# Attention by halves beside networks by quarters, the third network in two lanes, the last beside the end of the delta rule

## The chip, the core and the metric

The kernel runs on one core of a Trainium2 chip, in float32 nearly throughout. The metric is the device time of one execution, in microseconds. The engines are PE (matrix products; PEld is its weight load), DVE (elementwise work and reductions), ACT (functions and copies), POOL (a second elementwise engine) and SP, whose queue issues every DMA of this kernel.

## The reference, cut to what matters

`x` is 1024 rows of 256. Six stages follow each other; each reads what the one before wrote.

```python
x = x + 0.5 * net0(layernorm(x))      # ternary weights 704 wide, with scales
x = x + attention(layernorm(x))       # 16 heads of 128, 4 key heads, window of 64, rotary,
                                      # relu(softmax1 - lam * softmax2), renormalized
x = x + 0.5 * net0(layernorm(x))      # the same weights again
x = x + 0.5 * net1(layernorm(x))      # weights looked up: lut[idx], 688 wide
x = x + delta_rule(x)                 # 16 heads, a recurrence over the rows
x = x + 0.5 * net1(layernorm(x))
# net(y) = (silu(y Wg * sg) * (y Wu * su)) Wd * sd
```

Layer norm and network treat every row by itself. The attention of a row reads keys of the row itself and of 63 rows before it. The delta rule goes through the rows in order, for each head.

## The kernel before, in words

The rows lie in SBUF as 8 tiles of 128 (`x`). `xnT` holds them normalized and transposed, with 64 columns of padding ahead. A half is four tiles, 512 columns of `xnT`.

**Networks.** `layernorm` (L100) takes a half: `bn_stats` and `bn_aggr` on DVE, a square root on ACT (L110), a reciprocal, the scaled tile `xn` (L116), two transposes on PE for each tile and one copy (L122). `ffn` (L124) takes a half through six chunks of 128 hidden units: PE makes `pg` and `pu` with 512 columns each (L135), ACT takes Silu (L140 with the scales, L152 without) and DVE multiplies (L143 or L153). Then for each tile PE makes `po` out of six products of 256 columns (L160), and DVE adds half of it to `x` (L167). `pg` and `pu` have two PSUM banks each.

**Table weights.** `lut_weights` (L169) is a generator. For each of 14 blocks of index (344 or 256 columns) it issues a load of `ix` and then 19 DVE steps: bit masks (L184, L189), selections among two table values (L195) and predicated copies (L208). `lut_steps` runs some steps of it after each chunk of the first network and after each tile of the attention.

**Attention.** All values come first (L237), with shifted copies of them by DMA (L245, L247). Then four groups of heads follow. For each, the keys and four queries are projected (L253) and rotated for both halves (`rope`: DVE L262, L263, L265, POOL L266). Then come eight tiles: PE adds the window mask and the scores in a PSUM tile of two banks (L291, L302), DVE takes the maxima (L313) and negates them (L314), ACT makes the exponentials (L319), DVE the differences (L336), ACT the relu (L339), POOL the renormalization (L346), PE the transposes (L349), the product with the values `pa` (L354) and the output `po` (L365), and DVE adds to `x` (L372). `pa` and `po` have a bank each.

**Delta rule.** `delta_rule` (L509) begins with narrow projections of all rows (L566, L578). Then it works through 16 pairs of tiles (four groups of heads, four pairs each) in rounds: `prepare` two pairs ahead (L641 are its projections), `triangle` one ahead, `solve`, `invert` and `values` for the pair itself, `advance` and `emit` for the pair behind; `emit` ends with a sum into `x` (L1104). `weave` gives each of these lanes a stretch of the round, and orders their steps by it. Small transfers to and from DRAM on SP's queue stand between `triangle`, `solve` and `invert`.

**What sets the order.** The program's text gives each engine a list, and a scheduler of the tile framework, which has a timeline of its own, reorders it before it is built. A tile in a pool has a number of buffers; an instruction that takes one again waits for the last reader. The stages of before follow each other in the text: both halves of the first network, the whole attention, both halves of the second and third networks, the delta rule, both halves of the last network. The table weights of the third network are written to DRAM (L457) and read again at the end (L473).

Of the kernel before, what the change touches and what calls it, by code (L numbers as in the profile page):

```python
# [59 lines left out]

@with_exitstack
def macaron_kernel(ctx, tc, out, a):
    nc = tc.nc
# [17 lines left out]
    nc.vector.memset(ones, 1.0)  # L81

# [3 lines left out]
    def stage_pools(stack):  # L86

        pool = lambda name, bufs, **kw: stack.enter_context(
            tc.tile_pool(name=name, bufs=bufs, reuse_waits="tile", **kw)
        )  # L90
        return dict(
            ln=pool("ln", 4),
            lnp=pool("lnp", 2, space=PSUM),
            ffh=pool("ffh", 2),
            ffs=pool("ffs", 3),
            ffp=pool("ffp", 2, space=PSUM),
            ffo=pool("ffo", 2, space=PSUM),
        )

    def layernorm(pools, hf):  # L100

        lp = pools["ln"]
        mv = lp.tile([P, 4, 2], F32, name="mv")
        for i in range(4):
            st = lp.tile([P, 6], F32, name="st")
            nc.vector.bn_stats(st, x[:, 4 * hf + i, :])
            nc.vector.bn_aggr(mv[:, i, :], st)
        sd = lp.tile([P, 4], F32, name="sd")
        nc.vector.tensor_scalar_add(sd, mv[:, :, 1], LN_EPS)
        nc.scalar.activation(sd, sd, AF.Sqrt)  # L110
        rs = lp.tile([P, 4], F32, name="rs")
        nc.vector.reciprocal(rs, sd)
        for i in range(4):
            n = 4 * hf + i
            xn = lp.tile([P, D], F32, name="xn")
            nc.vector.tensor_scalar(  # L116
                xn, x[:, n, :], mv[:, i, 0:1], rs[:, i : i + 1], ALU.subtract, ALU.mult
            )
            pt = pools["lnp"].tile([P, KC, P], F32, name="pt")
            for c in range(KC):  # L120
                nc.tensor.transpose(pt[:, c, :], xn[:, c * P : (c + 1) * P], ident)
            nc.scalar.copy(xnT[:, :, PAD + n * P : PAD + (n + 1) * P], pt)  # L122

    def ffn(pools, hf, wg, wu, wd, inter, scaled):  # L124

        cols = slice(PAD + hf * 512, PAD + (hf + 1) * 512)
        hT = pools["ffh"].tile([P, NI, 512], F32, name="hT")
        for ic in range(NI):
            n = min(P, inter - ic * P)
            cs = slice(ic * P, ic * P + n)  # L130
            pg = pools["ffp"].tile([P, 512], F32, name="pg")
            pu = pools["ffp"].tile([P, 512], F32, name="pu")
            for w, ps in ((wg, pg), (wu, pu)):
                for c in range(KC):
                    nc.tensor.matmul(  # L135
                        ps[:n], lhsT=w[:, c, cs], rhs=xnT[:, c, cols], start=(c == 0), stop=(c == KC - 1)
                    )
            sg = pools["ffs"].tile([P, 512], F32, name="sg")
            if scaled:
                nc.scalar.activation(  # L140
                    sg[:n], pg[:n], AF.Silu, scale=pp[:n, C_GS + ic : C_GS + ic + 1]
                )
                nc.vector.scalar_tensor_tensor(  # L143
                    hT[:n, ic, :],
                    pu[:n],
                    pp[:n, C_US + ic : C_US + ic + 1],
                    sg[:n],
                    ALU.mult,
                    ALU.mult,
                )  # L150
            else:
                nc.scalar.activation(sg[:n], pg[:n], AF.Silu)  # L152
                nc.vector.tensor_mul(hT[:n, ic, :], pu[:n], sg[:n])  # L153
            lut_steps(1024)
        for i in range(4):
            t = 4 * hf + i
            po = pools["ffo"].tile([P, D], F32, name="po")
            for ic in range(NI):
# [4 lines left out]
                    rhs=wd[:n, ic, :],  # L163
# [3 lines left out]
            nc.vector.scalar_tensor_tensor(x[:, t, :], po, 0.5, x[:, t, :], ALU.mult, ALU.add)  # L167

    def lut_weights(pool):  # L169
# [7 lines left out]
        for src, dst in (("gate_idx", w1g), ("up_idx", w1u), ("down_idx", w1d)):  # L177
            for c in range(dst.shape[1]):
                for c0 in range(0, dst.shape[2], I1 // 2):
                    n = min(I1 // 2, dst.shape[2] - c0)  # L180
                    ix = pool.tile([P, n], I32, name="ix", tag="ix", bufs=2)
                    nc.sync.dma_start(out=ix, in_=a[src][c * P : (c + 1) * P, c0 : c0 + n])
# [30 lines left out]
    lut = iter(())  # L213

    def lut_steps(columns):

        while columns > 0:
            got = next(lut, None)
            if got is None:
                return  # L220
            columns -= got

    def attention(wpool):
        win = wpool["win"]
        with tc.tile_pool(name="aqk", reuse_waits="tile", bufs=2) as qp, tc.tile_pool(name="av", reuse_waits="tile", bufs=1
        ) as vp, tc.tile_pool(name="as", reuse_waits="tile", bufs=2) as sp, tc.tile_pool(name="asm", reuse_waits="tile", bufs=4
        ) as small, tc.tile_pool(name="ap", reuse_waits="tile", bufs=2, space=PSUM
        ) as pj, tc.tile_pool(name="asc", reuse_waits="tile", bufs=2, space=PSUM) as psc, tc.tile_pool(name="aout", reuse_waits="tile", bufs=1, space=PSUM
        ) as pao:


            v = vp.tile([P, 2 * NT, NKV * HD], F32, name="v")
            nc.gpsimd.memset(v[0:64, 0, :], 0.0)
            for n in range(NT):
                pv = pj.tile([P, 512], F32, name="pv", tag="pj")
                for c in range(KC):
                    nc.tensor.matmul(  # L237
                        pv,
                        lhsT=xnT[:, c, PAD + n * P : PAD + (n + 1) * P],
                        rhs=wpool["wv"][:, c, :],  # L240
                        start=(c == 0),
                        stop=(c == KC - 1),
                    )
                nc.scalar.copy(v[:, 2 * n + 1, :], pv)
                nc.sync.dma_start(out=v[64:128, 2 * n, :], in_=v[0:64, 2 * n + 1, :])  # L245
                if n < NT - 1:
                    nc.sync.dma_start(out=v[0:64, 2 * n + 2, :], in_=v[64:128, 2 * n + 1, :])  # L247

            def rope(dst, w, hcol, hf):

                pr = pj.tile([P, 512], F32, name="pr", tag="pj")
                for c in range(KC):
                    nc.tensor.matmul(  # L253
                        pr,
                        lhsT=w[:, c, hcol : hcol + HD],
                        rhs=xnT[:, c, PAD + hf * 512 : PAD + (hf + 1) * 512],
                        start=(c == 0),
                        stop=(c == KC - 1),
                    )
                cs = slice(hf * 512, (hf + 1) * 512)  # L260
                rot = sp.tile([P, 512], F32, name="rot")
                nc.vector.tensor_mul(rot[0:64], pr[64:128], wpool["sin"][64:128, cs])  # L262
                nc.vector.tensor_mul(rot[64:128], pr[0:64], wpool["sin"][0:64, cs])  # L263
                runs = lambda ap: ap.rearrange("p (w t) -> p w t", t=64)
                nc.vector.tensor_mul(dst, runs(pr), runs(wpool["cos"][:, cs]))  # L265
                nc.gpsimd.tensor_add(dst, dst, runs(rot))  # L266

            for g in range(NKV):
                kT = qp.tile([P, PAD + T], F32, name="kT")
                nc.gpsimd.memset(kT[:, 0:PAD], 0.0)  # L270

                qTs = []
                for hf in range(2):
                    qT = qp.tile([P, 2, NT, 2, 64], F32, name="qT", bufs=3)
                    qTs.append(qT)
                    kh = kT[:, PAD + hf * 512 : PAD + (hf + 1) * 512]
                    rope(kh.rearrange("p (w t) -> p w t", t=64), wpool["wk"], g * HD, hf)
                    for h in range(HG):
                        rope(
                            qT[:, h // 2, :, h % 2, :],  # L280
                            wpool["wq"],
                            (g * HG + h) * HD,
                            hf,
                        )
                lam = wpool["lam"][:, 2 * g : 2 * g + 2].unsqueeze(2).to_broadcast([P, 2, 2])
                for n in range(NT):


                    ps = psc.tile([P, 2, 4, P], F32, name="ps")
                    for s in range(2):  # L290
                        nc.tensor.matmul(  # L291
                            ps[:, s].rearrange("p b k -> p (b k)"),
                            lhsT=wpool["idb"],
# [92 lines left out]
    with tc.tile_pool(name="w0", bufs=1, side="right") as w0p:  # L386
# [12 lines left out]
        with tc.tile_pool(name="wa", bufs=1) as wap, tc.tile_pool(  # L399
# [24 lines left out]
            with ExitStack() as st:  # L424
                pools = stage_pools(st)
                for hf in range(2):
                    layernorm(pools, hf)
# [833 lines left out]
```

## Time and profile before

| | us |
|---|---|
| median of 3 runs (1783.14 to 1787.38) | 1785.18 |
| the profiled execution | 1795.66 |
| its span, first to last instruction | 1793.8 |
| PE busy | 1532.6 |
| DVE busy | 1186.9 |
| ACT busy | 831.3 |
| POOL busy | 526.4 |

Mean granted clock of PE over the span: 0.897.

The span is cut by first and last instructions of some lines:

| | begins | ends |
|---|---|---|
| first network, with its loads and norms | 0 | 109.0 (first L262) |
| attention, first rope to last sum | 109.0 | 439.4 (last L372) |
| second and third networks, narrow projections | 439.4 | 599.6 (first L641) |
| delta rule, first projection to last sum | 599.6 | 1731.2 (last L1104) |
| rest of the last network | 1731.2 | 1793.8 |

To read a row of a stretch: its two ends, its length, then busy time and count of instructions for PE, PEld, DVE, ACT and POOL, the granted PE clock (1.00 is full), the share of the DMA engines and GB/s. To read a row of a group: line, engine, operation, names of output and inputs with shapes, count, then busy time and mean ns of one, then the engine's idle time ahead of them and what ended it. One float32 matmul shows as two records. Busy times of one engine overlap by a few per cent where rows are added.

### The profile page before, as it was taken

Reading aid. Unit: us, or ns where it says so; the run is one execution under the profiler, and the core shown is the slowest. Engines: PE = TensorE matmul, PEld = TensorE weight load, DVE = VectorE, ACT = ScalarE, POOL = GpSimd, SP = SyncE. Lnnn points to the kernel's source line nnn. Section 1 sums busy time; section 2 is a strip of 40 time slices with the busy share of each in tenths; the row PEclk is TensorE's granted clock in tenths of the full one; section 3 lists DMA queues with packets and bytes.
Section 4 is the critical chain, followed back from the end, with each engine's and each line's share of the span. In section 5 each row is a group of like instructions: output and inputs, shape, how many; then the busy total and the mean of one; then the engine's idle time right before and its main releaser. Section 6 shows DMA issues by size and latency. Waiting matters only on the chain.

```text
span 1793.8 us, 33380 instructions
## 1 busy us (share of the span) xinstructions
PE 1532.6 (85%) x13152; PEld 1107.1 (62%) x13152; DVE 1186.9 (66%) x2569; ACT 831.3 (46%) x1981; POOL 526.4 (29%) x470
## 2 busy tenths in 40 slices
PE   7886868777999766789989889898999898998879
PEld 3434445545555555667767677677778776776745
DVE  3999977584232357667678678876768877877221
ACT  2117273746122344536645645654665564563320
POOL 0022223231001034335434434433434442543100
PEclk9997989889999766789889989989889988989989
DMA  7020000002002001021111121102120120111100
GB/s 241 32 54 26 3 19 1 1 1 66 0 0 47 1 7 23 10 52 28 24 15 43 21 56 22 30 12 44 38 50 15 22 47 9 40 24 23 56 0 24
DMA packets 150348, 54.94 MB, mean 31 GB/s; under 512 B 116784, under 2 KB 142704, under 8 KB 149936
## 3 DMA queue, kind: packets, MB, share of 16 engines
q1 hardware_dynamic: 150192, 52.81, 12.8%
q8 instruction: 104, 1.70, 0.4%
q14 instruction: 52, 0.43, 0.1%
HBM read 39.11 MB, written 11.70 MB: 28 GB/s over the span
## 4 chain that ended last, share of the span: by engine, by line
PE 41%; DVE 26%; ACT 11%; DMA 9%; issue 6%; POOL 4%; SPq 3%; another core or an unknown queue 1%; DVEq 0%; POOLq 0%; ACTq 0%
PE ps L641 5%; DMA dm<-ml 4%; PE po L160 4%; PE pg L135 3%; PE pu L135 3%; DVE kq L813 3%; ACT e L319 3%; PE pm L791 2%; PE pr L253 2%; DVE k L655 2%; PE pg L700 2%; PE px L1101 2%; DVE other L195 2%; PE po L365 2%; DVE other L208 2%
## 5 line engine op out<-in xcount | busy, mean ns | idle before, releaser
L819 POOL TENSOR_TENSOR k<-k,d 128x512 f32<-128x512 f32 x96 | 149.7, 1559 | 312.2 <-PE pm L791 190.6
L791 PE MATMUL pm<-kq,k 128*64 128x64 f32 x3072 | 133.5, 235 | 29.9 <-POOL kq L742 11.5
L791 PEld LDWEIGHTS pm<-kq,k 128*64 128x64 f32 x3072 | 113.3, 146 | 62.0 <-issue 40.0
L813 DVE TENSOR_TENSOR kq<-kq,d 128x1024 f32<-128x1024 f32 x96 | 130.8, 1363 | 17.8 <-PE pm L791 6.7
L319 ACT ACTIVATE e<-ps,nm 128x128 f32<-128x128 f32 x256 | 91.5, 397 | 63.6 <-DVE nm L314 62.3
L655 DVE SCALAR_TENSOR_TENSOR k<-ps,pp,k 128x256 f32<-128x256 f32 x192 | 84.7, 473 | 27.0 <-ACT k L653 25.5
L655 DVE SCALAR_TENSOR_TENSOR q<-ps,pp,q 128x256 f32<-128x256 f32 x192 | 86.2, 478 | 22.7 <-ACT q L653 20.0
L655 DVE SCALAR_TENSOR_TENSOR v<-ps,pp,v 128x256 f32<-128x256 f32 x192 | 87.5, 474 | 19.8 <-ACT v L653 18.5
L253 PE MATMUL pr<-xnT,wq 128*128 128x512 f32 x128 | 64.7, 641 | 22.1 <-DVE nm L314 10.6
L641 PE MATMUL ps<-xnT,wv 128*128 128x259 f32 x256 | 79.5, 439 | 2.7 <-DVE v L655 1.5
L983 PE MATMUL dz<-mz,zt 64*64 64x32 f32 x768 | 74.9, 230 | 8.0 <-ACT mz L976 8.0
L991 PE MATMUL dz<-zt,mz 64*64 64x32 f32 x1024 | 81.4, 234 | 0.0
L641 PE MATMUL ps<-xnT,wq 128*128 128x259 f32 x256 | 78.6, 442 | 0.4 <-DVE ss L681 0.2
L365 PE MATMUL po<-wo,oT 128*128 128x256 f32 x256 | 64.1, 394 | 13.7 <-ACT oT L362 12.4
L991 PEld LDWEIGHTS dz<-zt,mz 64*64 64x64 f32 x1024 | 67.3, 147 | 12.4 <-issue 10.6
L1101 PE MATMUL px<-wdo,oT 128*128 128x256 f32 x256 | 70.4, 421 | 5.1 <-ACT oT L1097 5.1
L641 PE MATMUL ps<-xnT,wk 128*128 128x259 f32 x256 | 71.8, 418 | 1.0 <-ACT k L653 0.5
L742 POOL TENSOR_TENSOR kq<-q,ge 128x1024 f32<-128x1024 f32 x16 | 51.3, 3209 | 70.3 <-PE pso L1073 40.0
L653 ACT ACTIVATE q<-ps,pp 128x256 f32<-128x256 f32 x64 | 30.4, 474 | 89.1 <-PE ps L641 86.5
L968 PE MATMUL pmz<-z,mt 64*64 64x64 f32 x1024 | 56.1, 233 | 18.0 <-DMA z<-z 13.7
L968 PEld LDWEIGHTS pmz<-z,mt 64*64 64x64 f32 x1024 | 42.9, 140 | 44.4 <-issue 17.8
L708 ACT ACTIVATE gy<-pg,pp 128x256 f32<-128x256 f32 x64 | 29.4, 474 | 85.4 <-PE pg L700 67.5
(215 smaller groups left out, 3953.5 us busy)
## 6 DMA issues: line engine op xcount, KB each, us to landing
zt<-zt SPq DMA_DIRECT2D x32, 256.0 KB
dm<-ml SPq DMA_DIRECT2D x64, 64.0 KB
z<-z SPq DMA_DIRECT2D x64, 64.0 KB
wq<-in_aWq SPq DMA_DIRECT2D x1, 2048.0 KB
wo<-in_aWo SPq DMA_DIRECT2D x1, 2048.0 KB
wk<-in_dWk SPq DMA_DIRECT2D x4, 512.0 KB
wq<-in_dWq SPq DMA_DIRECT2D x4, 512.0 KB
wv<-in_dWv SPq DMA_DIRECT2D x4, 512.0 KB
```

The lines of the kernel that those rows point to most:

```text
L135: nc.tensor.matmul(ps[:n], lhsT=w[:, c, cs], rhs=xnT[:, c, cols], start=(c == 0), stop=(c == KC - 1))
L253: nc.tensor.matmul(pr, lhsT=w[:, c, hcol : hcol + HD], rhs=xnT[:, c, PAD + hf * 512 : PAD + (hf + 1) * 512], start=(c == 0), stop=(c == KC ...
L319: nc.scalar.activation(e[:, s, j, :], ps[:, s, j, :], AF.Exp, bias=nm[:, 4 * s + j : 4 * s + j + 1], scale=SUB**-0.5, accum_out=z[:, s, j ...
L365: nc.tensor.matmul(po, lhsT=oT[:, h, :], rhs=wpool["wo"][:, g * HG + h, :], start=(h == 0), stop=(h == HG - 1),)
L641: nc.tensor.matmul(ps[:, 0 : 2 * P + 3], lhsT=w[nm][:, c, h * HD : (h + 1) * HD], rhs=xnT[:, c, PAD + t0 - 3 : PAD + t0 + 2 * P], start=(c ...
L655: nc.vector.scalar_tensor_tensor(yh, xi, pp[:, col : col + 1], yh, ALU.mult, ALU.add)
L791: nc.tensor.matmul(pm[half, :, c * HG + h, :].rearrange("p b (s l) -> p b s l", l=n), lhsT=k[:, c, h, half], rhs=rights(kq[:, :, c, h, half]),
L813: nc.vector.tensor_mul(kqr, kqr, dl.unsqueeze(1).unsqueeze(3).to_broadcast([P, 2, 2 * HG * runs, n]),)
L819: nc.gpsimd.tensor_mul(kl, kl, dr.unsqueeze(2).to_broadcast([P, 2 * HG * runs, n]))
L968: nc.tensor.matmul(pmz[half, c, h], lhsT=p["turn"][f"mt{n}"][half, c, h], rhs=z[half, c, h], start=True, stop=True,)
L991: nc.tensor.matmul(runs(dz[half, 1, c, h]), lhsT=mz[half, c, h], rhs=right(zt[half, c, h, half], n), start=True, stop=True,)
L1101: nc.tensor.matmul(px, lhsT=oT[:, h, :], rhs=u["w"]["o"][:, h, :], start=(h == 0), stop=(h == HG - 1))
```

## The change

- Networks and norms work by quarters (two tiles, 256 columns). `network` and `norm` are generators. The inverse root is a power on POOL in place of ACT's square root and DVE's reciprocal. Each transpose has its own copy.
- In the scaled network ACT makes a tanh and a scaled copy, DVE adds and multiplies the two in SBUF, and then multiplies by the gate in PSUM: two DVE and two ACT instructions for a chunk of 256 columns, where one of each stood for 512.
- Attention works by halves of rows: four groups for the first half, then four for the second. The keys' tail is carried over. Scores have three PSUM tiles of one bank each, with one maximum reduction for each (negated in the same instruction); `pa` and the output share one bank; projections and transposes share two. `wq` is scaled once, by ACT.
- `weave` and `chain` move to the top and order everything: quarters 0 and 1 of the first network with 60 steps of table weights; the first half of attention with quarters 2 and 3 and 70 steps; the second half with quarters 0 and 1 of the second network and the other steps.
- After attention, two lanes of four PSUM banks each do the rest of the second network, the third, the norm ahead of the delta rule and the narrow projections, which are cut by quarters too (class `Narrow`).
- The load of `wo` is behind the other attention weights. A load of `ix` waits for a POOL copy of one column of the tile of `x` that attention finished last (`pace`).
- The quarters of the last network are lanes in the last four rounds of the delta rule. Its weights come back from DRAM in buffers that the delta rule has done with. Each output tile is sent when it is done.

The core of the diff:

```diff
+        nc.vector.tensor_scalar_add(rs, mv[:, :, 1], LN_EPS)
+        nc.gpsimd.tensor_tensor(rs, rs, mhalf[:, 0:2], ALU.pow)
...
+            pgu = kit["ps"].tile([P, 2, 2 * P], F32, name="pgu", tag=kit["tag"], bufs=kit["banks"])
...
+                nc.scalar.activation(sg[:n], pgu[:n, 0], AF.Tanh, scale=half(0))
+                gu = kit["wide"].tile([P, 2 * P], F32, name="gu", bufs=2)
+                nc.scalar.mul(gu[:n], pgu[:n, 1], half(1))
                 nc.vector.scalar_tensor_tensor(
-                    hT[:n, ic, :],
-                    pu[:n],
-                    pp[:n, C_US + ic : C_US + ic + 1],
-                    sg[:n],
-                    ALU.mult,
-                    ALU.mult,
-                )
+                    sg[:n], sg[:n], 1.0, gu[:n], ALU.add, ALU.mult
+                )
+                nc.vector.tensor_mul(hT[:n, ic, :], pgu[:n, 0], sg[:n])
...
+                    if "by" in pace:
+
+                        nc.gpsimd.tensor_copy(ix[:, 0:1].bitcast(F32), pace["by"])
                     nc.sync.dma_start(out=ix, in_=a[src][c * P : (c + 1) * P, c0 : c0 + n])
...
+                ps = psum.tile([P, 4, P], F32, name="ps", tag="sc", bufs=3)
...
+                nc.vector.tensor_reduce(ns, ps, AX.X, ALU.max, negate=True)
...
+            pa = psum.tile([P, HG, 2, 64], F32, name="pa", tag="pa", bufs=1)
...
+            po = psum.tile([P, D], F32, name="poa", tag="pa", bufs=1)
...
+            weave(
+                (0.0, 0.9, 12, chain(network(kit("ff", 2), 0, w0, I0, scales), norm(kit("ff", 2), 0))),
+                (0.1, 1.0, 12, chain(network(kit("sc", 3), 1, w0, I0, scales), norm(kit("sc", 3), 1))),
+                (0.0, 1.0, 60, some(lut, 60)),
+            )
+
+            for c in range(KC):
+                nc.scalar.mul(wa["wq"][:, c, :], wa["wq"][:, c, :], SUB**-0.5)
+            carry = dict(v={}, k=atp.tile([P, NKV, PAD], F32, name="ktail"))
+            weave(
+                (0.0, 1.0, 84, attention(atp, psum, wa, 0, carry)),
+                (
+                    0.0,
+                    1.0,
+                    24,
+                    chain(
+                        *(
+                            stage
+                            for qr in (2, 3)
+                            for stage in (network(kit("ff", 2), qr, w0, I0, scales), norm(kit("ff", 2), qr))
+                        )
+                    ),
+                ),
+                (0.0, 1.0, 70, some(lut, 70)),
+            )
+            weave(
+                (0.0, 1.0, 84, attention(atp, psum, wa, 1, carry)),
+                (0.0, 1.0, 20, chain(*(network(kit("ff", 2), qr, w0, I0, scales) for qr in (0, 1)))),
+                (0.0, 0.9, 136, lut),
+            )
...
+            third = lambda tag, qr: chain(
+                network(kit(tag), qr, w1, I1), norm(kit(tag), qr), narrow.steps(kit(tag), qr)
+            )
+            weave(
+                (0.0, 0.9, 46, chain(third("fa", 0), third("fa", 1), second("fa", 3), third("fa", 3))),
+                (0.0, 0.7, 23, chain(second("fb", 2), third("fb", 2))),
+            )
...
-        for i in range(-2, len(pairs) + 1):
+        for i in range(-2, len(pairs) + 2):
...
+            qr = i - len(pairs) + 2
+            if qr == 0:
+                tw = table_weights((kdw, "wk", 1), (kdw, "wq", 1), (pre, "tmp", 1), (pre, "q", 1))
+            if qr >= 0:
+                lanes.append((0.2, 1.0, 10, network(kit, qr, tw, I1, to=xo)))
             weave(*lanes)
```

## The prediction

> **What bounds the kernel now.** I read the page's totals and its 40 slices first, then busy times cut at the stage seams, then the attention alone, then groups of instructions by form.
>
> ```profile
> PE 1532.6 (85%) x13152; PEld 1107.1 (62%) x13152; DVE 1186.9 (66%) x2569; ACT 831.3 (46%) x1981; POOL 526.4 (29%) x470
> ...
> PE   7886868777999766789989889898999898998879
> ...
> DVE  3999977584232357667678678876768877877221
> ...
> PEclk9997989889999766789889989989889988989989
> ```
>
> Each digit is the busy tenth of one slice of 44.8 us. No engine binds throughout: where DVE digits are 9 (slices 2 to 5) PE is not full, where PE is 9 (11 to 13) DVE has 2 to 4.
>
> ```profile
> 11.00:91.00 80.00, 73.21 (x228) 38.47 (x226) 57.89 (x152) 18.92 (x34) 0.66 (x1) 0.97 0.36 123
> 91.00:440.00 349.00, 264.97 (x1278) 168.37 (x1276) 273.08 (x680) 170.25 (x844) 87.98 (x76) 0.90 0.07 22
> 440.00:585.00 145.00, 138.94 (x424) 73.36 (x425) 44.06 (x123) 34.84 (x60) 5.01 (x15) 0.97 0.07 15
> 585.00:700.00 115.00, 78.39 (x588) 57.28 (x588) 60.11 (x111) 51.19 (x83) 32.20 (x27) 0.69 0.04 4
> ...
> 1705.00:1794.00 89.00, 73.36 (x240) 42.25 (x240) 19.03 (x39) 15.57 (x25) 4.09 (x4) 0.92 0.04 12
> ```
>
> Columns: stretch, length, busy PE, PEld, DVE, ACT, POOL, then granted clock, DMA share and GB/s. First network, attention, networks two and three, the delta rule's start, the end. The networks fill PE and leave DVE empty; attention needs both engines and fills neither. So a gain is there if the two are laid side by side, and its size is set by what both need together. The attention by its four groups of heads:
>
> ```profile
> 107.00:194.00 87.00, 60.57 (x286) 37.65 (x285) 84.85 (x220) 40.21 (x206) 23.01 (x19) 0.84 0.06 19
> 194.00:277.00 83.00, 61.12 (x304) 38.40 (x303) 66.59 (x165) 40.09 (x207) 22.17 (x19) 0.90 0.03 10
> 277.00:353.00 76.00, 60.33 (x315) 40.06 (x314) 52.28 (x127) 40.58 (x208) 21.20 (x18) 0.93 0.00 1
> ```
>
> The same columns; the first group also carries 42 us of table-weight work, the third none. With it DVE is full (84.85 of 87); without it no engine is, and a group takes 76 by the latency of its chain of scores, exponentials and products: 38 per half.
>
> Four groups of DVE work in attention (busy, mean ns, idle before): they price its tiles.
>
> ```profile
> L313 DVE TENSOR_REDUCE nm<-ps 128x8 f32<-128x1024 f32 x32 | 38.5, 1210 | 0.4 <-PE ps L302 0.3
> L336 DVE SCALAR_TENSOR_TENSOR d<-e,lw 128x128 f32<-128x128 f32 x128 | 41.7, 385 | 2.2 <-PE pd L349 0.5
> L262 DVE TENSOR_TENSOR rot<-pr,sin 64x512 f32<-64x512 f32 x40 | 27.7, 693 | 16.3 <-PE pr L253 15.5
> L372 DVE TENSOR_TENSOR x<-x,po 128x256 f32<-128x256 f32 x32 | 13.2, 414 | 19.9 <-PE po L365 19.9
> ```
>
> **Part by part**, by the marks of this profile: first rope on DVE (L262) at 109.0; last attention sum (L372) ends 439.4; first delta projection (L641) 599.6; last delta sum (L1104) ends 1731.2; the span is 1793.8. The changed program was built, not run; the order in which it lists each engine's instructions is what I count, and durations come from the rows of before.
>
> *To the first rope.* Loads stay in order but wo moves behind cos, sin and lam; the index load still follows them all, and DVE's first mask now stands (as at 40.5 before) near 41 with two chunks of the network behind it. Between it and the first rope DVE has 51 table steps of 0.46 (23.5), two chunks (1.7), four sums of 0.415 and six tiles' norms (6.4): 33, less 5% overlap. 41+31.5=72.5, so **−36.5**: two quarters of the network have moved later. ACT scales wq (two of 2048 columns, about 1.9 each by L716's 1.06 for 1024) in the middle of its network work, so seven chunk pairs wait for wq's landing. By the bytes ahead of it (6.8 of 10.8 MB by 40.5) that is near 26; five PSUM banks let PE run to about 32: nothing, up to +4. The power on POOL costs 1.01 (L1089) for a table load of 1.28 plus root. POOL's library instruction before the first one no longer has attention's 100 us of cover. The trace gives it no row. GPSIMD Engine Reference, "Instruction dispatch", prices a first call to freshly loaded code at about 6 us; no run here shows it. PE starts at 13.9 on the gate weights anyway, so I take 0, bound +4. The w0d product on POOL (1280 columns, 3 to 4 by L742) is done before PE wants it near 37.
>
> *Attention with four quarter networks.* DVE per tile and group of heads: two half reductions (0.68 each, an estimate: half of 1.21 and a start), four differences of 0.385, the small ones 0.97, the sum 0.414: 4.3, times 32=137. 40 ropes of 2.07 (two rows near 0.69 and the cosine's 0.692)=83. The negation (L314, 8.3) goes. A scaled quarter chunk costs DVE 0.415+0.41 where half of 0.744 stood, ACT about 0.4+0.45 where half of 0.687 stood. Table steps left: 92 us (14 blocks of 19 at 0.34 to 0.54 by the rows of L189, L195 and L208, less those 51). DVE's two for a quarter are estimates from L1091 (0.69 for 512 columns, both inputs in SBUF) and L372 (0.414 for 256 from PSUM). By the built order, the eight half groups hold DVE 45, 33, 40, 39, 52, 41, 44, 56 and PE 40, 41, 30, 32, 45, 42, 29, 39: the network sits in the first two of each half only. Overlap takes 7% off DVE (rows add to 295 where 273 were busy). Taking for each the largest of DVE×0.93/0.97, PE/0.9 and 38 gives 366; if neighbours smooth out, 340. I take 357, against 330.4: **+27**. Each table load now waits, through a one-column POOL copy, for a finished tile: with POOL at 88 of 349 the ropes and products behind that copy have slack, so 0, up to +10.
>
> *To the delta rule.* Six quarters remain: 36 matmuls of 256 columns each at 0.46 (L160: 24 records, two per matmul, in 5.8, or 0.43 in short runs)=99; ten norms' transposes 9; the narrow projections 9; and three seams of the last quarter (network, network, narrow) without filler, 4 each by the 4.19 that PE waited at 443.14: 130, against 160.2: **−30**. Ten norm table loads go; the first seam is covered, since quarters 0 and 1 are ready.
>
> Here a rule speaks against the change. TensorE: Matmul & The Clock Gate, "A second HAM failure mode", says that matmul groups cycling through PSUM banks leave small gaps that throttle the clock. The row of the third stage has 0.97 granted while cycling four banks. With 0.69 (the delta start's) instead, 117 of matmul work would take 170, and this stage +50. A quarter chunk occupies PE 1.8 and ACT and DVE 0.85 each, on four banks a lane, so I take the row.
>
> *Delta rule.* Same instructions, another interleaving; from 599.6 to 1731.2 it takes 1131.6. I take ±12 for the reordering. Into its end come three quarter networks (50 of PE), 2.2 MB of weights on SP's queue between the solver's small transfers, and 6 of DVE each. PE was busy 91.5 of 117 from 1614 to 1731, 10 of that the old last network: 35 free, so **+15** (0 if the low-clock idle absorbs all, +45 if nothing does). Behind a queued network chunk stands the recurrence (psr, pw, pn); every part of its chain waits.
>
> *The tail.* Before, the last delta sum and the first activation of the last half network that could follow it:
>
> ```profile
> 1730.80 0.42 DVE L1104 TENSOR_TENSOR x<-x,px 128x256 f32<-128x256 f32 x1 [0.59 <-PE px L1101]
> ...
> 1733.65 0.60 ACT L152 ACTIVATE sg<-pg 128x512 f32<-128x512 f32 x1
> ```
>
> 62.6 to the end. After: one quarter: norm 4.5 (0.43+0.18+0.15+1.01+0.42+0.6 and copies), 24×0.46=11, last chunk and outputs 7, out 3.2: 26. **−36.5**.
>
> Sum: −36.5+27−30+15−36.5=−61 on 1793.8, 1732.8. The profiled execution took 1795.66, 0.6% over the median; carried as a difference, 1785.18−61=**1724**.
>
> **Rivals.** *Attention packs fully* (0.18): DVE 325 busy at 97%, the first group's fill, is 335, and the delta end takes none: 1724−22−15=1687. For: that 84.85. Against: the eight half groups are uneven, and every network matmul is in four of them. *The delta end pays* (0.13): the three networks' 46 of PE lie wholly on the recurrence: +30, 1754. For: DVE and PE over 90% until 1638. Against: PE 19 of 34 after 1697. *Slower* (0.06): pa and poa now share one PSUM bank and scores have three banks for four. A tile's pa 0.86, copy 0.6, poa 1.72 and sum 0.41 then run in a row, 3.6 of a period of 11.2. It eats the gain once the period passes 13.1 (each hand-over late by some 0.6, about one table step); at 13.4 the time is 1794. For: ACT's oT waited 46 for pa already. Against: 7.6 of slack. *It doesn't do what it says* (0.02): if queues ran as before, seams only, within 0.2%.
>
> **Numbers.** Main case 0.61, 1705 to 1742. The range to 1680 and 1762 takes in the rivals next to it. Faster by over 0.2% (about what can be told from no change) 0.92, within 0.02, slower 0.06.
>
> **What would show it.** First rope at 66 to 80; attention's last sum 415 to 445; first delta projection 545 to 575; delta to its last sum 1135 to 1160; tail 24 to 30; clock over 0.9 in the network stage. Wrong if attention passes 420 in length, or the clock there falls under 0.85.

## The result and the profile after

The changed kernel takes 1800.45 us (median of 7 runs, 1793.21 to 1802.61); the kernel before, on the same chip, 1785.18. The ratio, taken over the runs and not from the two medians, is 1.0074, with the interval 1.0054 to 1.0094: slower by 0.7%, where 3.4% faster was forecast. The profiled execution took 1802.61 with a span of 1800.6. By the marks of the prediction:

| stage | before | forecast | after |
|---|---|---|---|
| to the first rope (L273) | 109.0 | 72.5 | 71.6 |
| attention, to its last sum (L373) | 330.4 | 357 | **429.0** |
| to the first delta projection (L693) | 160.2 | 130 | 126.4 |
| delta rule, to its last sum (L1156) | 1131.6 | 1146.6 | 1147.2 |
| tail | 62.6 | 26 | 26.4 |

Four of five came within 4 us. Attention, 72 us over its forecast, is the whole miss. The page's totals and slices (of 45.0 us each):

```profile
PE 1568.7 (87%) x13552; PEld 1204.0 (67%) x13552; DVE 1223.3 (68%) x2668; ACT 842.5 (47%) x2109; POOL 559.9 (31%) x506
...
PE   7799888998799866788998989899998998989996
...
DVE  2976678888743245786777768778777776868331
```

PE, at 6 to 8 in slices 4 to 10 before, now stands at 8 to 9 in slices 3 to 10, with DVE at 6 to 8. The first three stretches of the table, as rows:

```profile
0.00:71.60 71.60, 48.77 (x180) 33.62 (x180) 39.15 (x118) 19.80 (x48) 8.74 (x16) 0.90 0.48 157
71.60:500.60 429.00, 376.82 (x1575) 255.31 (x1575) 333.20 (x822) 195.94 (x919) 95.11 (x91) 0.89 0.06 17
500.60:627.00 126.40, 120.76 (x535) 92.95 (x536) 41.51 (x126) 31.68 (x100) 11.25 (x22) 0.95 0.13 35
```

DVE's 333 in attention is near the forecast's 350×0.93=325. PE's 377 is over its 298/0.9=331. Three groups of it in attention, and last the scores' row of the kernel before:

```profile
L316 PE MATMUL ps<-kT,qT 64*128 64x128 f32 x512 | 80.4, 328 | 9.3 <-POOL qT L276 9.3
...
L325 DVE TENSOR_REDUCE nm<-ps 128x4 f32<-128x512 f32 x64 | 42.8, 684 | 26.6 <-PE ps L316 26.5
...
L273 DVE TENSOR_TENSOR rot<-pr,sin 64x512 f32<-64x512 f32 x40 | 27.7, 693 | 19.8 <-PE pr L265 19.1
...
L302 PE MATMUL ps<-kT,qT 64*128 64x128 f32 x512 | 43.6, 316 | 0.0
```

The DVE rows are as costed (the half reduction 0.684 by an estimate of 0.68). The scores' PE time is not: 80.4 for the same 512 records that took 43.6, which is 37 of the 46 that PE has over. The change issues all four heads of one half of the array's rows and then of the other; the kernel before took the row halves in turn. The prediction priced them at the old row and did not see this. That this order lengthens attention was the first theory.

### The profile page after: what moved, and what is told of

It reads as the page before. It is cut to its first block, busy times and chain, and to the rows that moved or that the text cites. A ratio compares the mean times of both kernels' runs of the same rounds, so it can differ in the third digit from the quotient of the medians.

```text
span 1800.6 us, 34409 instructions
## 1 busy us (share of the span) xinstructions
PE 1568.7 (87%) x13552; PEld 1204.0 (67%) x13552; DVE 1223.3 (68%) x2668; ACT 842.5 (47%) x2109; POOL 559.9 (31%) x506
## 4 chain that ended last, share of the span: by engine, by line
PE 46%; DVE 22%; ACT 12%; issue 7%; DMA 6%; POOL 5%; SPq 1%; another core or an unknown queue 1%; DVEq 0%; POOLq 0%; ACTq 0%
PE pgu L144 7%; PE ps L693 5%; PE po L171 4%; PE pm L843 3%; PE ps L316 3%; DVE kq L865 3%; DMA dm<-ml 2%; PE pr L265 2%; DVE other L212 2%; PE px L1153 2%; PE pg L752 2%; DVE k L707 2%; POOL k L871 2%; PE poa L366 2%; PE pss L730 2%
## 5 line engine op out<-in xcount | busy, mean ns | idle before, releaser
L871 POOL TENSOR_TENSOR k<-k,d 128x512 f32<-128x512 f32 x96 | 158.7, 1654 | 279.2 <-PE pm L843 200.0
L843 PE MATMUL pm<-kq,k 128*64 128x64 f32 x3072 | 141.1, 240 | 35.3 <-DVE kq L865 13.6
L843 PEld LDWEIGHTS pm<-kq,k 128*64 128x64 f32 x3072 | 119.0, 150 | 70.5 <-issue 49.4
L316 PEld LDWEIGHTS ps<-kT,qT 64*128 64x128 f32 x512 | 68.0, 225 | 40.6 <-issue 28.5
L316 PE MATMUL ps<-kT,qT 64*128 64x128 f32 x512 | 80.4, 328 | 9.3 <-POOL qT L276 9.3
L276 POOL TENSOR_TENSOR qT<-qT,rot 128x512 f32<-128x512 f32 x32 | 42.7, 1334 | 127.1 <-DVE qT L275 110.2
L693 PE MATMUL ps<-xnT,wq 128*128 128x259 f32 x256 | 77.7, 439 | 3.5 <-issue 2.5
L120 POOL TENSOR_TENSOR rs<-rs,mhalf 128x2 f32<-128x2 f32 x24 | 17.3, 729 | 196.1 <-DVE rs L119 196.1
L346 POOL TENSOR_TENSOR d<-d,dz 128x512 f32<-128x512 f32 x32 | 35.1, 1097 | 133.3 <-DVE dz L345 82.6
L693 PE MATMUL ps<-xnT,wk 128*128 128x259 f32 x256 | 70.1, 414 | 6.1 <-DVE k L707 6.1
L693 PE MATMUL ps<-xnT,wv 128*128 128x259 f32 x256 | 73.8, 415 | 0.7 <-DVE qk L788 0.7
L366 PE MATMUL poa<-wo,oT 128*128 128x256 f32 x256 | 67.1, 408 | 6.5 <-ACT oT L363 6.4
```

Source lines behind the costliest of these rows:

```text
L316: nc.tensor.matmul(ps[:, j, :], lhsT=qT[s * SUB : (s + 1) * SUB, hp, 2 * i + r].rearrange("p h t -> p (h t)"), rhs=kT[s * SUB : (s + 1) * ...
L366: nc.tensor.matmul(po, lhsT=oT[:, h, :], rhs=w["wo"][:, g * HG + h, :], start=(h == 0), stop=(h == HG - 1),)
L693: nc.tensor.matmul(ps[:, 0 : 2 * P + 3], lhsT=w[nm][:, c, h * HD : (h + 1) * HD], rhs=xnT[:, c, PAD + t0 - 3 : PAD + t0 + 2 * P], start=(c ...
L843: nc.tensor.matmul(pm[half, :, c * HG + h, :].rearrange("p b (s l) -> p b s l", l=n), lhsT=k[:, c, h, half], rhs=rights(kq[:, :, c, h, half]),
L871: nc.gpsimd.tensor_mul(kl, kl, dr.unsqueeze(2).to_broadcast([P, 2 * HG * runs, n]))
```

## The experiments

All by the same marks. Ratios are to the kernel before on the same chip, with their intervals. "PE in it" is the busy time of PE in attention, and beside it stands the clock granted there. The planner is the scheduler that orders the program's text. The edits below are shortened.

| kernel | us | ratio | attention | PE in it, clock | delta rule |
|---|---|---|---|---|---|
| before | 1785.18 | | 330.4 | 247, 0.90 | 1131.6 |
| after | 1800.45 | 1.0074 (1.0054–1.0094) | 429.0 | 377, 0.89 | 1147.2 |
| e1 scores in turn | 1794.95 | 1.0061 (1.0037–1.0085) | 427.4 | 377, 0.88 | 1140.7 |
| e2 before, one row half first | 1796.17 | 1.0069 (1.0048–1.0090) | 327.2 | 265, 0.90 | 1141.0 |
| e3 poa in pj's banks | 1886.89 | 1.0589 (1.0549–1.0629) | 497.6 | 414, 0.81 | 1156.0 |
| e4 no pace | 1820.02 | 1.0215 (1.0179–1.0251) | 421.4 | 373, 0.90 | 1182.5 |
| e5 unwoven | 1804.83 | 1.0139 (1.0102–1.0177) | 386.0 | 327, 0.82 | 1135.1 |
| e6 unwoven, in turn | 1821.84 | 1.0258 (1.0215–1.0301) | 378.7 | 276, 0.88 | 1157.2 |
| e7 woven, in turn | 1770.19 | 0.9963 (0.9944–0.9983) | 398.9 | 332, 0.95 | 1141.5 |
| e8 e6 with own poa bank | 1812.89 | 1.0193 (1.0156–1.0230) | 383.8 | 279, 0.85 | 1143.9 |
| e9 before by halves | 1856.89 | 1.0404 (1.0362–1.0446) | 385.3 | 263, 0.80 | 1147.2 |
| e10 ropes early | 1754.24 | 0.9825 (0.9786–0.9864) | 391.9 | 327, 0.95 | 1147.0 |
| e11 ropes across halves | 1757.86 | 0.9838 (0.9805–0.9870) | 385.1 | 324, 0.97 | 1151.4 |
| e12 tables first | 1779.33 | 0.9969 (0.9949–0.9989) | 399.1 | 330, 0.94 | 1154.9 |
| e13 e7, one row half first | 1814.93 | 1.0185 (1.0137–1.0232) | 402.3 | 343, 0.94 | 1189.3 |
| e15 tables after | 1778.07 | 0.9960 (0.9941–0.9978) | 362.6 | 317, 0.98 | 1138.9 |
| e16 four score banks | 1781.00 | 0.9969 (0.9951–0.9986) | 394.4 | 345, 0.97 | 1162.5 |
| e17 own poa, 3 score banks | 1771.59 | 0.9913 (0.9882–0.9943) | 408.9 | 364, 0.92 | 1138.6 |
| e18 tables spread | 1809.41 | 1.0115 (1.0071–1.0159) | 374.0 | 322, 0.98 | 1214.7 |
| e19 one network bank | 1788.28 | 1.0000 (0.9972–1.0028) | 400.9 | 352, 0.94 | 1163.0 |

Read the attention column, not the times: none of e1 to e19 edits the delta rule (e18 moves transfers toward it), but DVE works through it in another order in every trace, as the planner built it, and it ran from 1135 to 1215 us, more than most edits are worth. A stage's length is that of one profiled execution. Stages whose program stays the same came within 3 us of each other (the third stage of the woven kernels with the tables ahead of it 123.5 to 126.4, the changed tail 25.4 to 27.0); attention itself was profiled once for each kernel, so a difference of a few us there shows nothing.

**The order of the scores: e1, e2, e13.** e1 swaps the two loops in the change, e2 in the kernel before:

```
-for s in range(2): for j in range(4): scores(s, j)      # the change
+for j in range(4): for s in range(2): scores(s, j)      # e1; e2 the other way round
```

> The changed kernel with its scores issued as before: both halves' banks opened, then head by head, row half 0 and row half 1 in turn, and after them the two reductions and the eight exponentials. Nothing left out. Theory (order of the scores): two matmuls in different row halves of the array overlap, two in the same do not, so L316's 80.4 us of PE in attention fall to about 44 (L302's 43.6 before), and with PE at 377 of 429 busy the attention shortens by 30 to 60: time 1740 to 1770. Rival (shared bank of pa and poa, or DVE, or POOL's pacing sets the period): PE's rows fall by 36 all the same, but the idle before pa and ps grows by as much: time 1790 to 1802.

> The kernel before with one edit: its scores row half by row half (all four heads of half 0, then of half 1) instead of in turn. Nothing left out. Theory: L302's 43.6 us of PE rise to about 80, but PE was at 247 of 330 in attention, so only part of it shows, and the chain of each tile grows by 1.2 us at least: 1795 to 1825. Rival (the order costs nothing): within 0.3% of 1785.

e1 didn't make the test: with three banks for the two halves of a tile, the planner kept one half's four heads together wherever the other half's bank was not yet free, and L317 stayed at 83.1 us (its score records stand in blocks of 8 or 24 between mask products, as in the change; before, in blocks of 16 or 32). e2 did. Its row in attention:

```profile
L302 PE MATMUL ps<-kT,qT 64*128 64x128 f32 x512 | 65.6, 321 | 2.5 <-issue 1.3
```

PE pays 22 us more than before's 43.6, and attention is 327.2 for 330.4: the order costs PE time and no length that shows. So e2's time of 1796, within the range that the theory gave it, doesn't bear the theory out: in the profiles its stages ahead of the delta rule are 6 us shorter and the delta rule is 9 longer. e13 repeats it in the woven kernel, on e7's two-bank tile:

> The kernel of e7 with one edit: inside the same two-bank tile the scores go row half by row half again; banks, reduction and the network's one bank stay. Nothing left out. Theory (the order takes PE's time when PE is filled by woven networks): PE in attention rises from 332 to about 365 and attention from 399 to 420 to 430. Rival (the banks or the one reduction of 1024 gave e7's 30 us): PE rises as well, but attention stays within 395 to 405, as e2's did.

402.3 for 398.9, with 11 us more of PE. The first theory has fallen. e7's 1770 lay in the range that it gave, and for another reason: e7 also took a bank from the woven networks.

**Banks and pacing as first rivals: e3, e4.**

```
-po = psum.tile([P, D], F32, name="poa", tag="pa", bufs=1)
+po = psum.tile([P, D], F32, name="poa", tag="pj", bufs=2)     # e3
-if "by" in pace:                                              # e4: the copy to ix falls away
```

> The changed kernel with the output product poa moved out of the one bank that it shares with pa into the two banks of pj, which pr, pv and pd use. Nothing left out. Rival of the prediction (pa and poa in one bank set the period of 13.4): the waits of pa for the sum L373 (4.6 us in sum) go and the period falls, time 1770 to 1790. Theory (order of the scores): only those 5 us of idle are there to be had, time 1793 to 1803, or more where pj's other users now wait.

> The changed kernel without the one-column POOL copy that holds each load of table indices until a tile of attention is done. Nothing left out. If POOL waiting in that copy for DVE's sum (22.3 us idle, 7 times) delays the ropes and products queued behind it, time 1780 to 1795. Theory (order of the scores): POOL is at 95 of 429 busy, and the 9.3 us that PE waits for POOL's qT sum are all that could go: 1793 to 1803.

e3 made it far worse: attention takes 69 us more, and rot's wait for pr, which now shares its banks with poa, rose from 19.1 to 28.3. e4 takes 8 off attention and the delta rule gives 35 back; the 1780 to 1795 that its removal might have brought did not come. Neither explains the 72 us.

**Weaving and halves: e5, e6, e8, e9.** e5 takes the networks out of attention, e6 puts scores into a two-bank tile, twice, with one reduction, and e8 gives poa its bank:

```
-weave(attention half 0, networks of quarters 2 and 3, tables)
+weave(first network, quarters 0 and 2 | 1 and 3, tables); weave(attention half 0, tables)   # e5
+ps = psum.tile([P, 2, 4, P], F32, name="ps", tag="sc", bufs=2)                              # e6
+po = psum.tile([P, D], F32, name="poa", tag="poa", bufs=1)                                  # e8
```

> The changed kernel with the four quarter networks taken out of attention: quarters 2 and 3 of the first network stand ahead of it beside 0 and 1, quarters 0 and 1 of the second behind it in the third stage. Scores stay row half by row half in three banks. Nothing left out. Theory (PE is the bound: the change added some 54 us of PE work ahead of the delta rule, and weaving got back about half): the networks' 83 us of PE come back as length outside attention, attention itself falls to 345 to 375, time 1795 to 1830. Rival (weaving itself costs, by the collisions of queues): 1765 to 1790.

> The kernel of e5 with one edit: a tile's scores in one tile of two PSUM banks, twice, issued in turn between the row halves, with one reduction of 1024, as before the change. Nothing left out. Theory (order of the scores costs PE up to 37 us, 12 us of time in e2): 12 to 30 us under e5, attention about 330. Rival (the order costs nothing here, since without networks PE has room): within 4 us of e5.

> The kernel of e6 with poa in a bank of its own beside pa, as before the change. Nothing left out. If the shared bank holds the tiles' chain back, 4 to 12 us under e6; if not, within 3 us of it. As its stages then are the kernel before's up to the delta rule, with the changed end, the sum of the steps gives 1760 to 1775.

None came where it was expected (345 to 375, about 330, and for e8 the stages of before). Without any network, attention takes 386, 379 and 384, whatever banks and order: some 50 more than before, with the same products. e6 has 51 us less of PE in it than e5 and is 7 shorter. What still differs from before is the halves, the ropes laid among the tiles, the pacing and a larger share of table steps (DVE 284 in e5 for 255). e9 puts only the halves into the kernel before:

```
-for g in range(NKV): ropes of both halves; for n in range(NT): tile
+for hf in range(2): for g in range(NKV): ropes of hf; for n in range(4*hf, 4*hf+4): tile
```

> The kernel before with one edit: attention goes half by half of the tokens, four groups of four tiles twice, instead of four groups of eight tiles (the keys' last 64 columns of the first half are kept per group). Nothing left out, nothing woven. Theory (group changes): between two groups no tile ends for 39 to 49 us before, and for 26 us between half groups in e8; eight fills instead of four lengthen the attention from 330 to 370 to 385, with PE's and DVE's work unchanged. Rival (halves cost nothing, the 50 us of e8 over before come from pacing, the interleaved ropes or the larger share of table steps): attention 325 to 340. The delta rule, untouched, has ranged from 1132 to 1182 by its built order, so the stage is what counts; the time would be 1820 to 1840 by the theory, 1780 to 1795 by the rival.

385.3, +55, with PE up only 16 and DVE down 7. The halves alone cost what the unwoven kernels lost. The third group of before, whole and in two parts, and then a half group of e9 and its two parts (all without table steps):

```profile
294.20:370.10 75.90, 60.23 (x313) 39.90 (x312) 52.19 (x127) 40.58 (x208) 21.27 (x19) 0.93 0.00 1
333.00:370.00 37.00, 32.73 (x153) 23.01 (x152) 21.23 (x56) 17.99 (x84) 9.42 (x9) 1.00 0.00 1
370.00:409.00 39.00, 27.20 (x162) 16.79 (x161) 31.07 (x72) 22.88 (x127) 11.93 (x10) 0.87 0.00 1
```

```profile
271.20:317.80 46.60, 34.10 (x156) 22.97 (x156) 25.16 (x63) 20.55 (x105) 10.44 (x10) 0.78 0.00 1
271.00:300.00 29.00, 16.73 (x93) 11.48 (x94) 15.47 (x47) 17.71 (x100) 5.51 (x5) 0.66 0.00 1
300.00:317.50 17.50, 17.26 (x63) 11.49 (x63) 9.59 (x17) 2.83 (x5) 4.84 (x4) 0.97 0.00 0
```

A half group is 46, not half of 76. In before the eight sums of that group end at 333 to 370 (37 us) and the next group's first at 409: 39 us in which no tile ends. In e9 four end in 17 us (254 to 271), and the next at 300: 29 us. So the part with the sums halves, and the part without them falls by a quarter only, and there are twice as many of those. In e9 the sums come with PE full (17.3 of 17.5) and ACT all but idle (2.8). In the 29 us ACT makes the half group's exponentials and PE works 16.7, at a clock of 0.66: as the planner ordered it, one engine waits for the other in turn. In before 19 of a group's 64 exponentials lie in the 37 us of sums, beside the products of other tiles. PE's waits ahead of the window mask, which opens a score tile, show it over the whole attention, in before and in e9:

```profile
L291 PE MATMUL ps<-win,idb 128*128 128x512 bf16 x60 | 21.2, 441 | 22.5 <-ACT e L319 19.1 <-DVE dz L345 3.2
L287 PE MATMUL ps<-win,idb 128*128 128x512 bf16 x45 | 22.1, 556 | 67.3 <-ACT e L315 53.4 <-DVE dz L341 14.0
```

Of the 55, how much is this and how much the lower clock (0.80 over e9's attention, 0.90 before) stays open; PE's busy time rose by 16.

**Which part of e7 helped: e7, e16, e17, e19.** e7 is the change with e6's scores; the banks came from the woven networks:

```
-kit("ff", 2)
+kit("ff", 1)                      # e7, e13, e16, e17, e19
-tag="sc", bufs=3
+tag="sc", bufs=4                  # e16; e17: poa in a bank of its own; e19: neither
```

> The changed kernel, woven as it is, with the scores of e6 (four banks) and only one bank for the networks woven into attention. Nothing left out. Theory: PE in attention falls from 377 to about 340 and the time to 1755 to 1785; what is left over the forecast is PE's idle. Rival (the order is not it, the period is set by latency and banks): 1790 to 1830, with PE's idle in attention up by 30 or more.

> The changed kernel with four single score banks instead of three, the fourth taken from the networks woven into attention (one bank left to them); order of the scores and the two reductions of 512 as the change has them. Nothing left out. Theory (a fourth score bank lets the next tile's second half in before the exponentials of the first are done): attention 395 to 410 where the change had 429. Rival (the one reduction gave the 30 us): attention 420 to 432.

> The changed kernel with three score banks as it has them, one bank for the woven networks, and the freed bank given to poa beside pa. Nothing left out. If the fourth score bank is what counts: attention 420 to 435. If the networks' single bank (they push in less eagerly) or the bank shared by pa and poa is: 395 to 412, and e16 will have fallen as well in the first case, not in the second.

> The changed kernel with one PSUM bank instead of two for the networks woven into attention, and the freed bank left empty: three score banks, pa and poa in one (in the first stage the lane of quarter 0 uses the two banks that the ropes use later). Nothing left out. If the receiver of the bank gives the gain in e16 and e17: attention 425 to 440. If the networks' single bank gives it (their matmuls push in less in front of the tiles' chain): 395 to 412. The time is read by this stage, as the delta rule's length has changed by up to 80 us with the built order.

398.9, 394.4, 408.9, and 400.9 with the bank left empty. So the receiver gives little (394 with the bank to the scores; 409, which is no gain, with it to poa); it is the networks' second bank that cost 28 us. Where the gate and up matmuls of the woven networks ran, after and e19 (stretch, length, PE busy with them alone, then the clock):

```profile
71.00:111.00 40.00, 11.44 (x48) 0.95 0.13 38
111.00:151.00 40.00, 9.62 (x43) 0.84 0.00 1
151.00:191.00 40.00, 1.38 (x7) 0.97 0.02 5
191.00:231.00 40.00, 0.00 (x0) 0.81 0.00 0
231.00:271.00 40.00, 0.00 (x0) 0.79 0.02 5
```

```profile
71.00:111.00 40.00, 7.77 (x32) 0.96 0.13 38
111.00:151.00 40.00, 3.94 (x16) 1.00 0.02 5
151.00:191.00 40.00, 6.93 (x29) 0.91 0.00 1
191.00:231.00 40.00, 4.94 (x21) 1.00 0.02 5
231.00:271.00 40.00, 0.00 (x0) 0.96 0.07 19
```

With two banks the planner runs the networks ahead, eight matmuls at a time: up to its first group's last output product PE has made 71 of the 72 of the first half, and nearly none is left for the gaps behind. With one bank they come by fours, 36, 16 and 20 in the first three groups, and the clock holds at 0.91 to 1.00. The first group's last sum ends at 166 in after and at 147 in e19; from there to the end of the half both take about as long (136 and 133). So the crowded work lengthens the group it stands in, and the groups without it don't get shorter. All six kernels with one bank and the tables in place lie at 394 to 409 unless their ropes were moved; after, e1 and e4 with two at 421 to 429, and e3, with poa among the ropes' banks, higher still. That the spreading is what helps, and not something else the single bank does, is read from the trace and was not tried apart.

**What bounds the rest: e10, e11, e12, e15, e18.** e10, e12 and e15 are edits to e7, e11 is one to e10, and e18 one to e11:

```
-next(steps, None)
+for _ in range(2): next(steps, None)                              # e10
+steps = rotated(0, ahead, 1)   # e11: half 1's first ropes in half 0's last group; half 0's networks by 0.55 of it
+for _ in lut: pass             # e12 ahead of attention, e15 behind it
+(0.0, 1.0, 76, lut)            # e18: e11, 76 steps beside the second network's last quarters
```

> The kernel of e7 with one edit: two rope steps of the next group after each tile instead of one, so that the last rope stands ahead of the group's last tile and not behind it. Nothing left out. Theory (group changes): PE's waits for POOL's qT (10.0 us in e7) go, and the next group's scores come sooner: attention 375 to 390 where e7 had 399, time 1745 to 1762. Rival (PE and DVE rows alone set it): attention 395 to 402, time within 5 us of e7.

> The kernel of e10 with the first ropes of the second half issued among the tiles of the first half's last group, and the networks of quarters 2 and 3 placed earlier for it (by 0.55 of the first half instead of its end). Nothing left out. Theory: the 31 us without an attention sum between the halves (281 to 312 in e7) shrink to some 15: attention 360 to 380, time 1730 to 1752. Rival: as e10, or longer, as the filler is now gone from the first half's last groups.

> The kernel of e7 with all table-weight steps put ahead of attention, so that attention carries none of their 92 us of DVE. Nothing left out, only moved; the first rope comes some 90 us later. If DVE bounds the woven attention: 399 falls to 340 to 365. If PE with its 332 us does: 385 to 399. If neither alone (both share the tiles' chain): 365 to 385.

> The kernel of e7 with the table-weight steps that stood in attention (but those of the first index loads) put behind it; their index loads wait for attention's last sum. Nothing left out, only moved; the third stage grows by up to 80 us, so only the attention stage is to be compared. If DVE's load bounds the woven attention: DVE there falls from 328 to about 245 and 399 to 345 to 365. If the tiles' own chain and the group changes with PE's 332 do: 385 to 400, with DVE's idle taking the difference. Between: both.

> The kernel of e11 with about half of the second half's table steps (76) taken out of attention and laid beside the two quarters of the second network that open the third stage, where DVE is at 41 of 125; the third network's quarters follow in two lanes. Nothing left out. By e15's rate (36 us of attention for 70 of DVE) attention falls from 385 to 362 to 376, and the third stage grows by 5 to 20: time 1738 to 1760. If the third stage grows by as much as attention falls, within 5 us of e11.

Earlier ropes give 7 (e10), and with the second half's first ropes too 14 (e11), less than was expected of both: the gap between the halves went from 31 us in e7 to 23 in e11, not to 15, and PE's waits for qT even rose in e10, from 10.0 to 16.8. e12 told nothing: the planner let the table steps slide back, and DVE kept 326 us in attention. e15 held them. Attention of e7, then attention and third stage of e15:

```profile
70.60:469.50 398.90, 332.07 (x1581) 218.46 (x1579) 327.75 (x795) 191.74 (x920) 95.71 (x91) 0.95 0.07 20
```

```profile
69.30:431.90 362.60, 316.67 (x1569) 211.60 (x1582) 257.25 (x605) 191.85 (x922) 90.75 (x81) 0.98 0.04 11
431.90:615.70 183.80, 135.02 (x535) 100.32 (x536) 109.01 (x315) 31.76 (x99) 13.31 (x32) 0.79 0.15 43
```

70 us less on DVE are 36 less of attention, though DVE was at 82% only (the index loads and their POOL copies left with the steps); and 59 more of the third stage, where PE now waits for the table weights. e18 is 11 shorter than e11 in attention at no such price (374.0, third stage 124.4), then loses more in a delta rule of 1214.7 us at a clock of 0.85. Whether that is the built order or the later transfers of the table weights stays open. e10 and e11 are the best kernels here, 1.7% and 1.6% under the kernel before; their intervals overlap.

## Why the prediction was wrong

- *To the first rope, −36.5*: right, −37.4. The first use of POOL's power, bounded at +4, cost nothing that shows: POOL's library instruction stands at 1.6 us and the first power begins at 5.5, when DVE hands over, so the 6 us weighed there don't fit in between; the first two powers took 1.51 us together, little more than later ones (0.70 each).
- *Attention, +27*: **the failed step**; it was +98.6. Two terms of its sum failed.
  - The floor of a half group: "a group takes 76 by the latency of its chain of scores, exponentials and products: 38 per half". e9 measured 46 for a half group, and +55 for the eight. Of the 76, the 37 us with the sums halve, and the 39 ahead of them go down to 29.
  - The maximum: "the largest of DVE×0.93/0.97, PE/0.9 and 38" takes work beside the chain as free up to the largest. By its own figures it comes to 359, not 366; with 46 in place of 38 it is 380, still 49 under the 429. The networks' 77 us of PE (L144 and L171) were mostly hidden with one bank, so that part of the idea was sound, but they cost 15 (e5's 386 to e19's 401). Their second bank, which the sum did not weigh, cost 28 more (401 to 429): crowded into the first group they made it longer, and the later groups did not give that back. And e15's 70 us of DVE were worth 36 of length, with DVE busy for 82% only.
  - From kernel to kernel: the halves 55 (before to e9), all other edits to attention but the networks 1 (e9 to e5), the networks with one bank 15, their second bank 28, together 99. That is a path through kernels and no division of the change's own trace. There the stretches between the half groups' sums are shorter than e9's (153 us in all for 206; before 127), and the sums within the half groups stand further apart (215 us in all for 132; before 140), since ropes and networks lie among the tiles.
- *To the delta rule, −30*: right, −33.8. The rule weighed there (the Trainium skill, TensorE: Matmul & The Clock Gate, "A second HAM failure mode"), which the page tells of one bf16 kernel with 512 columns, didn't bite on float32 products of 256: the clock was 0.95 while four banks a lane were cycled, as the row of 0.97 said.
- *Delta rule, +15*: +15.6, but with 1135 to 1215 among kernels that changed nothing in it, the hit is partly luck; ±12 was too narrow.
- *Tail, −36.5*: right, −36.2.
- *The rivals*: "slower", at a period of 13.4 us a tile, named the very period (429.0/32) by luck, for its reasons were wrong: a bank of its own for poa did not help (409 for e19's 401 in e17, 384 for e6's 379 in e8), and a fourth score bank gave 7 at most (e16). Both were tried with one network bank or none, not beside the change's two. "Packs fully" was far off: PE was busy for 88% of attention, but with scores at 80 for 44 and at a clock of 0.89. The sign given for failure, "attention passes 420 in length", is what came.

## What to carry to other kernels

Before a loop is split so that other work can be laid beside it, count its fills, the stretches at the start of a group in which nothing of it ends: here they fell by a quarter when the group was halved, and doubled in number. Measure the split alone, without the weaving. A filler should come in small pieces that last to the end of the stage it fills; fewer buffers for it can spread it better than more, as one bank here did (401 for 429). And where a planner orders the instructions, compare stages, not whole times, since an untouched stage can move by several per cent.

## What was not expected of the hardware

Matmuls of 64 rows that alternate between the two row halves of the array take PE 43.6 us per 512 records, in one half after the other 65.6 (e2), at the same clock of 0.90; e7 and e13 repeat it, 41.7 and 57.9, at 0.95 and 0.94. Of the 511 starts that follow another, 256 come within 20 ns of it when they alternate, and 87 in e2. No length was gained by it: attention moved by 3 us in either pair. The granted clock fell to 0.80 in e9's attention, with PE busy for 263 of 385 us, where the same products had 0.90 at 247 of 330; within a half group it was 0.66 where PE had 16.7 of 29 us and 0.97 where it had 17.3 of 17.5.
